# Four layers on one core: Strassen's scheme for the keys and queries of layer 0, first values in layer 3's lone step, and a new order at the end of layer 2

## The chip, the cores and the metric

The kernel runs on one core of a Trainium2 chip. The core has a matrix engine (TensorE, PE in the profile; PEld is its weight load), a vector engine (VectorE, DVE), a scalar engine (ScalarE, ACT), GpSimd (POOL) and SyncE (SP), which here issues the DMA transfers. Each engine works through its own queue in order, and the queues wait for one another by semaphores. Matrix products go into PSUM, everything else lies in SBUF. The metric is the time of one execution on the device in microseconds (us), lower is better.

## The reference

The input x has 4 images of 512 channels and 64 x 64 pixels, float32. Four layers follow one another, each keeping the shape:

```python
# layer 0: attention over the 4096 pixels, D = 64
t = einsum('oc,bchw->bohw', w_qkv, x)            # key, query, value: 64 rows each
attn = softmax(einsum('bdk,bdq->bkq', key, query), axis=1)
x0 = scale * einsum('oc,bchw->bohw', w_out, einsum('bdk,bkq->bdq', value, attn)) + x
# layer 1: 8 experts, mixed per image by a router of the mean over pixels
rw = sigmoid(x0.mean(axis=(2, 3)) @ router_w.T + router_b)
out = relu(bn(conv1x1(x0, mix(w1, rw)))); out = relu(bn(conv3x3(out, mix(w2, rw))))
x1 = relu(bn(conv1x1(out, mix(w3, rw))) + x0)
# layer 2: linear attention
Q, K, V = softplus(Wq x1 + bq), softplus(Wk x1 + bk), Wv x1 + bv
norm = 1.0 / einsum('bnm,bm->bn', Q, K.sum(-1) + EPS)
x2 = x1 + gamma * einsum('bnm,bmc,bn->bcn', Q, einsum('bmn,bcn->bmc', K, V), norm)
# layer 3: 1024 projected channels, half of them scanned along rows and columns
gate, scan = split(einsum('bchw,oc->bohw', x2, w_proj) + b_proj)
x3 = x2 + gamma * gate * sigmoid(cumsum_discounted(cumsum_discounted(scan, rows), columns))
```

Layer 0's projection is the matrix product of the 128 key and query rows (512 channels deep) with the 4096 pixels of an image.

## The kernel before, in words

The program goes through the four images ("batches") one after the other, and in each through `layer0` to `layer3`. An image is held in SBUF as four "pairs" `xs[0]` to `xs[3]` of 1024 pixels; each pair is a tile of 128 partitions by 4 channel blocks (`kc`) by two halves of 512 pixels. Five such places exist (`xpool`); the fifth serves in turn as part of attention's ring, for expert weights, and for layer 3's weights. PSUM is used in two forms: `pair_psum` (three buffers of two banks) and `bank` (two buffers of one bank). SBUF buffers rotate too: `four`, `block` and `bigp`.

PE's program order is the order of the code everywhere, since the whole loop lies in a manual schedule for PE. DVE's order is that of the code where `tc.manual_schedule` names DVE (parts of layers 0, 1 and 2) and in layer 3, where it is so for ACT too. Elsewhere a scheduler orders DVE and ACT by their dependences.

**Layer 0** (L191 to L408). `project_in` (L206) multiplies a 64-column piece of `wqkv_sb` with a pair, the two halves of 512 pixels into the two 64-partition halves of a bank, side by side in the array. Per pair the loop at L220 issues keys and queries (`kq`), four ACT copies of the keys into both partition halves (L229), a DVE copy of the queries (L230), the values (`vv`), a DVE copy (L234) and, one pair later, four transposes of them (L215). Then attention runs in groups: scores (L248), exponentials by ACT into a ring of tiles (L251), running sums by DVE (L256), and products with the values (L263) one group behind. The mean over pixels that the router needs comes for pairs 2 and 3 from ACT activations into a `junk` tile with an accumulated sum (L325). At the end out-products (L307) and additions of the result to x (`add_out`, L312) alternate with the mixing of expert weights.

**Layer 1** (L410 to L527) mixes the remaining expert weights (`mix`, and `mix_by_expert` on DVE, which is called at its start for `ex10`) and runs the three convolutions; `conv3` ends in DVE additions to x (L518).

**Layer 2** (L529 to L693). `features(w, pair)` makes key (w = 1) or query (w = 0) features of two pairs in PSUM (L543); `softplus` (L547) takes ACT's Abs, Relu (`pos`, L552), Exp and Ln and DVE operations. `key_transpose` (L571) turns the keys, `move` (L583) turns pieces of x by eight transposes (L588) and a copy, and `products` (L595) multiplies the two into `g` (L605), with moves and products alternating one by one. `normed` (L637) makes the denominators of one pair: a product of the queries with `kbd` (L640), a reciprocal (L642), a multiplication (L645). After the products come a copy of `g` to `gsb` by ACT (L664), a fold of the two halves by PE (`gk`, L668), another ACT copy (`gt`), the product with Wv (L677) and `kv` by DVE (L678). `value_product` (L687) and `value_add` (L692) then give x2 piece by piece; all but the first four pieces of them are spread over layer 3.

**Layer 3** (L717 to L906) computes its projection already by Strassen's scheme over blocks of 2 x 2: seven products per block, sums of x (`sum_x`, L748) and of the weights ahead of them, a copy of one product into the bank of another as its start value (`seed`, L774), and copies `e2`, `e3` (L778). It runs in nine steps of one loop (L866): in step i the scan half of tile i ("s"), the gate half of tile i − 1 ("g") and the late work of the last tile ("l": scans along rows, a turn, scans along columns, a sigmoid) are interleaved by the table `steps` (L856). Step 0 has no gate half and the last step no scan half: the last is the "lone step", with a table of its own, `last_steps` (L861). A pair of the next image is loaded every second step (L905). The last additions go out by `add_x` (L848) and a DMA on SP.

At the start the four pairs of batch 0 are loaded, pair 0 in four pieces (L86), and then the other constants. GpSimd scales `wv_sb` and `bv_sb` (L112, L113); `kbd`, a 128 x 128 block matrix, is cleared (L130); `bn_s` and its kin are made from the parameters (L136 to L145).

Of the kernel before, what the change touches and what calls it, by code (L numbers as in the profile page):

```python
# [45 lines left out]
def unshifted(ctx: ExitStack, tc: tile.TileContext, fits, x, wqkv_t, wout_t, router_t,  # L46
# [6 lines left out]
    xpool = ctx.enter_context(tc.tile_pool(name="xpool", bufs=5))  # L53
# [26 lines left out]

    def load_pair(b, pr):

        t = xpool.tile([P, KC, 2 * NB], F32, tag="x", name=f"x_{b}_{pr}")
        src = x[b, :, pr * 2 * NB:(pr + 1) * 2 * NB].rearrange("(kc p) n -> p kc n", p=P)
        if b == 0 and pr == 0:
            for kc in range(KC):  # L86
                nc.sync.dma_start(t[:, kc, :], src[:, kc, :])
        else:
            nc.sync.dma_start(t, src)
        return t  # L90
# [4 lines left out]
    xs = [load_pair(0, pr) for pr in range(NPAIR)]  # L95
    prm_sb = const.tile([P, NPRM], F32, tag="prm", name="prm_sb")
# [32 lines left out]
    kbd = const.tile([P, P], F32, tag="kbd", name="kbd")  # L129
    nc.gpsimd.memset(kbd, 0.0)  # L130

# [33 lines left out]
    def load_experts(b, j, n, pool, tag, pack=True):  # L165
        if pack:
            ex = pool.tile([P, n, 4, 2, P], F32, tag=tag, name=f"ex_{b}_{j}")
            nc.sync.dma_start(ex, packed[:, j:j + n])
        else:
            ex = pool.tile([P, n, E, P], F32, tag=tag, name=f"ex_{b}_{j}")  # L170
            nc.sync.dma_start(ex, experts[j:j + n].rearrange("n p e c -> p n e c"))
        return b, j, n, ex
# [18 lines left out]
    def layer0(b, xs):  # L191
# [8 lines left out]
        ring4 = bigp.tile([P, 4, 2, NB], F32, tag="big", name=f"ring_{b}")  # L200
        ringx = xpool.tile([P, 4, 2, NB], F32, tag="x", name=f"ringx_{b}")
        ring = [ring4[:, i] for i in range(4)] + [ringx[:, i] for i in range(4)]
        ring += [four(f"ring_{b}_{i}") for i in range(8, RING)]
        pool_acc = small.tile([P, KC, NPAIR], F32, tag="pool_acc", name=f"pool_{b}")

        def project_in(y, col0, pr):  # L206
            for kc in range(KC):
                for h in range(2):
                    nc.tensor.matmul(y[h * D:(h + 1) * D, :], wqkv_sb[:, kc, col0:col0 + D],  # L209
                                     xs[pr][:, kc, h * NB:(h + 1) * NB], start=kc == 0, stop=kc == KC - 1)  # L210

        def v_transpose(pr, vv, vsb):
            tr = vv[:, 1, :].rearrange("p (j c) -> p j c", c=P)
            for j in range(TPB):
                nc.tensor.transpose(tr[:, j, :], vsb[:, j * P:(j + 1) * P], ident)  # L215
            t0 = pr * 2 * TPB
            nc.vector.tensor_copy(
                vt[:, t0:t0 + 2 * TPB, :].rearrange("p (h j) d -> p j h d", h=2),
                tr.rearrange("p j (h d) -> p j h d", h=2))

        pend = None
        for pr in range(NPAIR):
            kq = pair_psum(f"kq_{b}_{pr}")
            project_in(kq[:, 0, :], 0, pr)
            project_in(kq[:, 1, :], D, pr)
            for h in range(2):
                n0 = (2 * pr + h) * NB
                for to in range(2):
                    nc.scalar.copy(key[to * D:(to + 1) * D, n0:n0 + NB], kq[h * D:(h + 1) * D, 0, :])  # L229
            nc.vector.tensor_copy(qry[:, pr * NB:(pr + 1) * NB], kq[:, 1, :])  # L230
            vv = pair_psum(f"vv_{b}_{pr}")
            project_in(vv[:, 0, :], 2 * D, pr)
            vsb = block(f"vsb_{b}_{pr}")
            nc.vector.tensor_copy(vsb, vv[:, 0, :])  # L234
            if pend is not None:
                v_transpose(*pend)
            pend = (pr, vv, vsb)
# [84 lines left out]
        junk = four(f"junk_{b}")  # L322
        for pr in range(NPAIR - 2, NPAIR):
            for kc in range(KC):
                nc.scalar.activation(flat(junk), xs[pr][:, kc, :], AF.Copy, accum_out=pool_acc[:, kc, pr:pr + 1])  # L325
# [3 lines left out]
        for g, group in enumerate(groups):  # L329
            for i in group:  # L330
                scores(i)
            if g == 0:
                v_transpose(*pend)
# [36 lines left out]
        with tc.manual_schedule(engines={mybir.EngineType.DVE}):  # L370
# [30 lines left out]
            for m in range(1, KC):  # L401
                add_out(pr, m, ys[m])
            for m in range(KC):
# [3 lines left out]
        return wcq, sel, rw, ex4, ex7, ex10  # L407

    def layer1(b, xs, wcq, sel, rw, ex4, ex7, ex10):
# [5 lines left out]
        mix_by_expert(wc, rw, ex10)  # L415
# [23 lines left out]
        v14 = xpool.tile([P, 4, HW // 4], F32, tag="x", name=f"v14_{b}")  # L439
# [89 lines left out]
    def layer2(b, xs, sums_of_six, mix_last, conv2, conv3, wcq, qs):  # L529

        ks = small.tile([P, NPAIR], F32, tag="ks", name=f"ks_{b}")
        g = bank(f"g_{b}", (P, C))
# [4 lines left out]

        def features(w, pair):
            z = pair_psum(f"z_{b}_{w}_{pair[0]}")
            for i, pr in enumerate(pair):  # L540
                for kc in range(KC):
                    for h in range(2):
                        nc.tensor.matmul(z[h * D:(h + 1) * D, i, :], wqk_sb[:, kc, w * D:(w + 1) * D],  # L543
                                         xs[pr][:, kc, h * NB:(h + 1) * NB], start=kc == 0, stop=kc == KC - 1)
# [37 lines left out]

        def move(pr, j):  # L583
# [11 lines left out]
        def products(pr, between=()):  # L595
            between = list(between)
            for j in range(TPB):
                t = pr * TPB + j
                if j + 2 < TPB:
                    move(pr, j + 2)  # L600
                elif between:
                    between.pop(0)()
                xt = moved.pop(0)
                for h in range(2):
                    nc.tensor.matmul(g[h * D:(h + 1) * D, :], kts[pr][:, j, h * D:(h + 1) * D], xt[:, h, :],  # L605
                                     start=t == 0, stop=t == NPAIR * TPB - 1)
# [18 lines left out]
        conv3(2, h2[2])  # L625
        rest = features(0, (0, 1))
        with tc.manual_schedule(engines={mybir.EngineType.DVE}):
            key_transpose((0, 1))
            rest()()
        for step in ahead(0):  # L630
            step()
        conv3(3, h2[3])
        products(0, ahead(1))
        weights[2]()
        features(1, (2, 3))()()
        products(1, ahead(2))
        rest = features(0, (2, 3))  # L637
        def normed(pr, between=None):
            den = bank(f"den2_{b}_{pr}")
            nc.tensor.matmul(den, kbd, qs[:, pr, :], start=True, stop=True)  # L640
            nrm = block(f"nrm_{b}_{pr}")
            nc.vector.reciprocal(nrm, den)  # L642
            if between:
                between()
            nc.vector.tensor_tensor(qs[:, pr, :], qs[:, pr, :], nrm, ALU.mult)  # L645

        with tc.manual_schedule(engines={mybir.EngineType.DVE}):
# [4 lines left out]
            for h in range(2):  # L652
                r = slice(h * D, (h + 1) * D)
                nc.vector.tensor_scalar(kbd[r, r], ones[r, 0:D], ksum[r, :], 1e-6, ALU.mult, ALU.add)
            key_transpose((2, 3))
            rest = rest()
            normed(0)
            rest()
        products(2, ahead(3))

        normed(1)
        products(3, [lambda: normed(2)])
        g_sb = block(f"gsb_{b}", (P, C))
        nc.scalar.copy(g_sb, g)  # L664

        gk = pair_psum(f"gk_{b}")
        for kc in range(KC):
            nc.tensor.matmul(gk[:, 0, kc * P:(kc + 1) * P], g_sb[:, kc * P:(kc + 1) * P], fold,  # L668
                             start=True, stop=True)
        gt = block(f"gt_{b}", (P, KC, P))  # L670
        nc.scalar.copy(gt, gk[:, 0, :].rearrange("p (kc c) -> p kc c", c=P))
        kvp = gk[:, 1, :]
        kv = small.tile([P, C], F32, tag="kv", name=f"kv_{b}", bufs=1)

        def make_kv():
            for kc in range(KC):
                nc.tensor.matmul(kvp, gt[:, kc, :], wv_sb[:, kc, :], start=kc == 0, stop=kc == KC - 1)  # L677
            nc.vector.scalar_tensor_tensor(kv, bv_sb, ksum, kvp, ALU.mult, ALU.add)  # L678

        with tc.manual_schedule(engines={mybir.EngineType.DVE}):  # L680
            normed(3, make_kv)
# [11 lines left out]
        return value_product, value_add, weights, wcq  # L693

    def load_quarters(b):
# [3 lines left out]
        sx = xpool.tile([P, 4, 2, 2, 2 * P], F32, tag="x", name=f"sx_{b}")  # L699
# [17 lines left out]
    def layer3(b, xs, value_product, value_add, weights, wcq):  # L717
# [32 lines left out]
        class Block:  # L750
# [3 lines left out]
            def __init__(self, kind, i):  # L754
# [5 lines left out]
                self.e = {}  # L760

            def product(self, k):
                if k == 1:
# [63 lines left out]
        class Gates(Block):  # L827
# [18 lines left out]
            def add_x(self, i):  # L846
# [10 lines left out]
                 ("s5", "l turn 0", "a"), ("g5", "l columns 1"),  # L857
# [4 lines left out]
        last_steps = (("g1", "g seed", "l rows 1", "l rows 0"), ("g5",), ("g6", "g copy_out 2", "l turn 1"), ("g2",),  # L862
                      ("g7", "g copy_out 3", "l columns 1", "g fourth", "l turn 0", "l columns 0", "l sigmoid 1",
                       "l sigmoid 0"), ("g4",), ("g3", "g third", "g first", "g second"))
        ys = [(pr, m) for pr in range(1, NPAIR) for m in range(KC)]
        nxt = []  # L866
        with tc.manual_schedule(engines={mybir.EngineType.DVE, mybir.EngineType.Activation}):
            for m in range(KC):
                value_add(0, m, value_product(0, m))
                if m == 1:  # L870
                    sum_x(0, 0)
            for part in range(1, 4):
# [3 lines left out]
            for i in range(len(tiles) + 1):  # L876
                who = {"l": last, "s": Sums(1, i) if i < len(tiles) else None, "g": Gates(0, i - 1) if i else None}
                made = None
                for step in steps if who["s"] else last_steps:
                    for what in step:  # L880
# [11 lines left out]
                        elif name == "a":  # L892
                            if made:
                                value_add(*made, y)
                                made = None
                        elif name == "t":
# [470 lines left out]
```

## Time and profile before

Three runs took 2716.63, 2718.47 and 2719.44 us. The profiled execution has a span of 2717.1 us, with a mean granted TensorE clock of 0.997.

| what | where | busy us in the span | mean ns of one |
|---|---|---|---|
| scores | PE L248 | 469.1 | 603 |
| running sums | DVE L256 (two ring forms) | 381.7 + 205.5 | 1223 |
| keys and queries | PE L209, kq | 116.2 | 607 |
| reciprocals of layer 2 | DVE L642, 16 of them | 53.7 | 3356 |
| key copies | ACT L229 | 37.0 | 579 |
| mean over pixels | ACT L325 | 33.9 | 1058 |

A row of the profile's groups gives the line, the engine, the operation, what it writes and reads, the shapes, how often it comes, the busy time and the mean of one, and then the idle time of the engine in front of the group and what ended it. Matmuls in float32 show two records each, and their records overlap, so the time of a run of matmuls is read from the start of one run to the start of the next in the timeline. In the list of waits a row names the waiting engine and line, the engine and line that ended the wait, and then the total, the number of waits and the longest.

### The profile page before, as it was taken

To read this page: it belongs to the slowest core of one execution; us is meant where nothing else is said; L and a number is where in the kernel's file an instruction comes from. 1 tells how busy PE (TensorE), PEld (TensorE's weight loads), DVE (VectorE), ACT (ScalarE), POOL (GpSimd) and SP (SyncE) were. 2 spreads that over 40 slices of the span, in tenths; PEclk is the share of its full clock that TensorE was granted. 3 is DMA by queue.
4 is the path that set the end of the run, shared out by engine and by line. 5 is a ranking of instruction groups with operands and counts; after the bars stand their busy time and mean duration, and the time that the engine had idled before them with its cause. 6 is when DMAs were issued, how large, how long until landed. Compare 5 with 4: busy or idle time off the path is not lost.

```text
span 2717.1 us, 25649 instructions
## 1 busy us (share of the span) xinstructions
PE 2667.3 (98%) x10046; PEld 1114.7 (41%) x10046; DVE 1961.2 (72%) x2197; ACT 1306.6 (48%) x1483; POOL 10.7 (0%) x26
## 2 busy tenths in 40 slices
PE   8999999999999999999999999999999999999998
PEld 3333364344333345444433334544443333554443
DVE  2688766787468876678747778667874777866787
ACT  4544354445555535345555453535555555352545
POOL 1000000000000000000000000000000000000000
PEclk9999999999999999999999999999999999999999
DMA  5000200021200020002220002001121000200011
GB/s 188 1 1 0 101 31 1 16 108 74 82 1 1 1 101 31 1 24 101 78 78 1 1 1 101 32 0 60 64 108 47 1 1 1 101 31 1 31 47 48
DMA packets 34545, 115.15 MB, mean 42 GB/s; under 512 B 2928, under 2 KB 12144, under 8 KB 32880
## 3 DMA queue, kind: packets, MB, share of 16 engines
q1 hardware_dynamic: 34416, 113.43, 11.1%
q8 instruction: 81, 1.33, 0.2%
q14 instruction: 48, 0.39, 0.0%
HBM read 79.86 MB, written 33.55 MB: 42 GB/s over the span
## 4 chain that ended last, share of the span: by engine, by line
PE 86%; DVE 9%; ACT 2%; DMA 1%; issue 1%; SPq 1%; DVEq 0%; ACTq 0%
PE s L248 17%; PE av L263 17%; PE sx L769 14%; PE zy L769 11%; PE c L444 4%; PE kq L209 4%; PE c L493 3%; PE c L516 2%; PE z L543 2%; PE wv L687 2%; PE vv L209 2%; PE g L605 2%; PE xtr L588 2%; PE c2e L493 2%; PE y L307 1%
## 5 line engine op out<-in xcount | busy, mean ns | idle before, releaser
L248 PE MATMUL s<-qv,key 64*128 64x512 f32 x2048 | 469.1, 603 | 1.8 <-ACT ring L251 1.8
L256 DVE TENSOR_TENSOR acc<-acc,ring 128x1024 f32<-128x1024 f32 x312 | 381.7, 1223 | 100.7 <-ACT ring L251 71.9
L251 ACT ACTIVATE ring<-s 128x1024 f32<-128x1024 f32 x336 | 317.7, 1038 | 224.1 <-PE s L248 224.0
L263 PE MATMUL av<-ring,qv 128*64 128x512 f32 x1344 | 304.5, 595 | 0.0
L248 PEld LDWEIGHTS s<-qv,key 64*128 64x128 f32 x2048 | 189.4, 187 | 274.8 <-issue 173.2
L256 DVE TENSOR_TENSOR acc<-acc,ringx 128x1024 f32<-128x1024 f32 x168 | 205.5, 1223 | 102.8 <-ACT ringx L251 90.2
L251 ACT ACTIVATE ringx<-s 128x1024 f32<-128x1024 f32 x176 | 172.1, 1040 | 207.0 <-PE s L248 207.0
L769 PE MATMUL sx<-t,sx 128*128 128x512 f32 x512 | 236.9, 597 | 0.0
L263 PEld LDWEIGHTS av<-ring,qv 128*64 128x64 f32 x1344 | 93.3, 137 | 198.6 <-issue 198.6
L263 PE MATMUL av<-ringx,qv 128*64 128x512 f32 x704 | 167.2, 598 | 0.0
L774 ACT COPY zy<-sx 128x512 f32<-128x512 f32 x64 | 36.5, 570 | 240.1 <-PE sx L769 230.6
L819 DVE TENSOR_TENSOR_SCAN t<-sx,t 128x512 f32<-128x512 f32 x128 | 148.8, 1210 | 1.7
L769 PEld LDWEIGHTS sx<-t,sx 128*128 128x128 f32 x512 | 95.9, 190 | 127.8 <-issue 121.1
L808 ACT COPY t<-s 128x1024 f32<-128x1024 f32 x64 | 127.2, 1994 | 40.5 <-DVE s L802 40.5
L778 ACT ACTIVATE e<-sx,prm_sb 128x512 f32<-128x512 f32 x128 | 86.9, 686 | 123.8 <-PE sx L769 123.8
L802 DVE TENSOR_TENSOR_SCAN s<-wc,s 128x512 f32<-128x512 f32 x128 | 146.0, 1204 | 0.0
L825 ACT ACTIVATE s<-t 128x1024 f32<-128x1024 f32 x64 | 125.5, 1987 | 1.0 <-DVE t L819 0.9
L769 PE MATMUL sx<-t,wq 128*128 128x512 f32 x256 | 117.0, 598 | 7.5 <-ACT e L778 7.5
L209 PE MATMUL kq<-x,wqkv_sb 128*64 128x512 f32 x512 | 116.2, 607 | 6.3 <-DMA x<-in_x_dram 5.6
L769 PE MATMUL zy<-t,wq 128*128 128x512 f32 x256 | 118.7, 604 | 2.5 <-ACT zy L774 2.5
L769 PE MATMUL zy<-x,wq 128*128 128x512 f32 x256 | 116.2, 594 | 0.0
L769 PE MATMUL sx<-x,wq 128*128 128x512 f32 x256 | 116.2, 594 | 0.0
(195 smaller groups left out, 3390.0 us busy)
## 6 DMA issues: line engine op xcount, KB each, us to landing
out_dram<-s SPq DMA_DIRECT2D x64, 512.0 KB, 2.6
x<-in_x_dram SPq DMA_DIRECT2D x15, 2048.0 KB, 8.5
ex<-in_packed_dram SPq DMA_DIRECT2D x8, 1536.0 KB, 6.3
ex<-in_packed_dram SPq DMA_DIRECT2D x4, 2048.0 KB, 7.9
ex<-in_experts_dram SPq DMA_DIRECT2D x4, 2048.0 KB, 7.9
wq<-in_wproj_t_dram SPq DMA_DIRECT2D x32, 256.0 KB, 4.5
ex<-in_experts_dram SPq DMA_DIRECT2D x4, 1536.0 KB, 7.1
x<-in_x_dram SPq DMA_DIRECT2D x4, 512.0 KB, 6.3
```

What stands on the lines that cost most here:

```text
L209: nc.tensor.matmul(y[h * D:(h + 1) * D, :], wqkv_sb[:, kc, col0:col0 + D], xs[pr][:, kc, h * NB:(h + 1) * NB], start=kc == 0, stop=kc == K ...
L248: nc.tensor.matmul(s[:, h, :], key[r, kt * P:(kt + 1) * P], qry[r, pr * NB:(pr + 1) * NB], start=True, stop=True)
L251: nc.scalar.activation(p, s, AF.Exp)
L256: nc.vector.tensor_tensor(accs[pr], accs[pr], p, ALU.add)
L263: nc.tensor.matmul(avs[pr][h * D:(h + 1) * D, :], vt[:, kt, :], ring[i % RING][:, h, :], start=kt == 0, stop=kt == NT - 1)
L444: nc.tensor.matmul(y[:, h, :], wc[:, kc, :], xs[pr][:, kc, h * NB:(h + 1) * NB], start=kc == 0, stop=kc == KC - 1)
L493: nc.tensor.matmul(y[:, lo - a:hi - a], u, v[:, lo:hi], start=dy == 1, stop=dy == 2)
L769: nc.tensor.matmul(y, w[:, c, self.kind, self.j * P:(self.j + 1) * P], v[:, c, :], start=c == 0 and k in (1, 5), stop=c == 1, skip_group_c ...
L802: nc.vector.tensor_tensor_scan(self.half(i, h), along[:, self.j + 2 * i, :], self.half(i, h), 0.0, ALU.mult, ALU.add)
L808: nc.scalar.copy(self.t[i].rearrange("p (w r) -> p w r", w=W), self.s[i].rearrange("p (r w) -> p w r", w=W))
L819: nc.vector.tensor_tensor_scan(th, down[:, i, :], th, 0.0, ALU.mult, ALU.add)
L825: nc.scalar.activation(self.s[i].rearrange("p (r w) -> p w r", w=W), tw, AF.Sigmoid)
```

## The change

The diff has five parts.

- Keys and queries of layer 0 are computed by Strassen's scheme over two pairs at once, the weights and the pixels in 2 x 2 blocks: seven products in the place of eight (class `Projections`, which keeps the steps as lists of words, as layer 3 does). `sum` makes sums of x (t5, t6, t7, t4 for pairs 0 and 1; n5 to n4 for pairs 2 and 3), `sum_weights` those of the weights, and "seed", "e2", "e3", "c11", "c12", "c21" and "c22" are the copies and additions around the products. Values are projected, copied (by ACT now) and turned in between.
- The value projection of the next image's pair 0 (v0) goes into the lone step of layer 3, and its sums t5 and t7 into step 7. The order of g1 and g5 in the lone step is exchanged. The last pair of the next image is loaded inside the lone step, into the fifth place. In batch 0, pair 1 is loaded in four pieces too.
- The activations for the mean over pixels write in place and are issued from inside the attention groups' code; `mix_by_expert` for `ex10` is called at the end of layer 0, after the `add_out` calls.
- The end of layer 2: `move` and `products` in twos; one moved piece in single banks (`move_by_halves`); the key features of pairs 2 and 3 right after `conv3(3)`; denominators of two pairs in 32-row tiles with one reciprocal (`invert`) and a product that spreads them (`divide`); weight sums later; `kv` in two halves.
- The query features of pairs 2 and 3 are cut into quarters: two lie around the copies of `g`, two after it, and they, their softplus and their division (`left`) are carried out in layer 3's first values and steps (`first_steps` and the word "q").

```diff
+    class Projections:
...
+        def steps(self, b):
+            first = "v1 cp01 v2 5 1 seed t6 t4 n5 6 e2 2 c11 n6 tr01 7 e3 c22 v3a n7 4 c21 3 c12 n4"
+            if b == 0:
+                first = "zero v0 1 seed t5 v1 cp01 t6 5 2 c11 t7 t4 n5 6 e2 n6 tr01 v2 7 e3 c22 v3a n7 4 c21 3 c12 n4"
+            return first.split(), "5 1 seed 6 e2 2 c11 v3b cp23 7 e3 c22 tr23 4 c21 3 c12".split()
...
+                elif step.isdigit():
+                    k = int(step)
+                    to = y if k in (1, 6, 7, 4) else zy[:, 0 if k == 2 else 1, :]
+                    for c in range(2):
+                        for h in range(2):
+                            nc.tensor.matmul(to[h * D:(h + 1) * D, :], self.w[k][:, c, :],
+                                             self.term(xs, pair, k, c)[:, h * NB:(h + 1) * NB],
+                                             start=c == 0 and k in (1, 5), stop=c == 1,
+                                             skip_group_check=k not in (1, 5))
+                elif step == "seed":
+                    nc.scalar.copy(zy[:, 0, :], y)
...
-        junk = four(f"junk_{b}")
-        for pr in range(NPAIR - 2, NPAIR):
-            for kc in range(KC):
-                nc.scalar.activation(flat(junk), xs[pr][:, kc, :], AF.Copy, accum_out=pool_acc[:, kc, pr:pr + 1])
+
+        def pool(pr, kc):
+            xm = xs[pr][:, kc, :]
+            nc.scalar.activation(xm, xm, AF.Copy, accum_out=pool_acc[:, kc, pr:pr + 1])
...
+            if 1 < g < 2 + 2 * KC:
+                pool(NPAIR - 2 + (g - 2) // KC, (g - 2) % KC)
...
                 add_out(pr, m, ys[m])
+            mix_by_expert(wcq, rw, ex10)
...
+        def invert(pair):
+            den = bank(f"den2_{b}_{pair[0]}")
+            for i, pr in enumerate(pair):
+                nc.tensor.matmul(den[32 * i:32 * (i + 1), :], kbd, qs[:, pr, :], start=True, stop=True,
+                                 tile_position=(0, 32 * i))
+            inv = block(f"inv_{b}_{pair[0]}")
+            nc.vector.reciprocal(inv[0:D, :], den[0:D, :])
+            return inv
...
+            g_sb = block(f"gsb_{b}", (P, C))
+            nc.scalar.copy(g_sb, g)
+            gt = block(f"gt_{b}", (P, KC, P))
+
+            late = (0, (2, 3), pair_psum(f"z_{b}_0_2"))
+            feature_part(*late, 0, 0, 2)
...
+        left = [lambda: feature_part(*late, 1, 0, 2), lambda: feature_part(*late, 1, 2, 2),
+                lambda: left.append(softplus(*late)), lambda: left.pop()(),
+                lambda: left.append(invert((2, 3))), lambda: divide((2, 3), left.pop())]
...
-        last_steps = (("g1", "g seed", "l rows 1", "l rows 0"), ("g5",), ("g6", "g copy_out 2", "l turn 1"), ("g2",),
+        first_steps = (("s1", "s seed", "q"), ("s5", "q"), ("s6", "s copy_out 2"), ("s2", "s first", "q"),
+                       ("s7", "s copy_out 3", "s fourth", "y"), ("s4", "s third", "a", "d"), ("y", "a", "q"),
+                       ("s3", "s second"))
+        last_steps = (("g5", "l rows 1", "l rows 0"), ("g1", "g seed"), ("g6", "g copy_out 2", "l turn 1"), ("g2",),
                       ("g7", "g copy_out 3", "l columns 1", "g fourth", "l turn 0", "l columns 0", "l sigmoid 1",
-                       "l sigmoid 0"), ("g4",), ("g3", "g third", "g first", "g second"))
+                       "l sigmoid 0", "v"), ("g4",), ("g3", "x", "g third", "g first", "g second"))
```

## The prediction

> **What bounds the kernel now.** I read the engines' busy times first, then the chain that ended last, then TensorE's (PE's) waits, then the timelines of the stretches that the diff touches.
>
> ```profile
> PE 2667.3 (98%) x10046; PEld 1114.7 (41%) x10046; DVE 1961.2 (72%) x2197; ACT 1306.6 (48%) x1483; POOL 10.7 (0%) x26
> PE 86%; DVE 9%; ACT 2%; DMA 1%; issue 1%; SPq 1%; DVEq 0%; ACTq 0%
> ...
> L209 PE MATMUL kq<-x,wqkv_sb 128*64 128x512 f32 x512 | 116.2, 607 | 6.3 <-DMA x<-in_x_dram 5.6
> ```
>
> PE is busy 98% of 2717.1 us at a full clock and its program order is fixed, so time is won in two ways: fewer matmuls, or less waiting in that order. The third line holds the key and query projections.
>
> ```profile
> PE sx L769 <- ACT e L778: 7.5, 12, 0.8
> PE kq L209 <- DMA x<-in_x_dram: 5.6, 1, 5.6
> PE xtr L588 <- ACT pos L552: 3.9, 4, 1.1
> PE wv L687 <- DVE kv L678: 3.7, 4, 0.9
> PE wo_t L161 <- DVE wot_sb L159: 3.2, 1, 3.2
> PE gk L668 <- ACT gsb L664: 2.7, 4, 0.7
> PE zy L769 <- ACT zy L774: 2.5, 4, 0.7
> PE y L307 <- DVE x L312: 2.4, 4, 0.6
> ```
>
> Total, times and longest of each wait: all of PE's waits come to some 37 us, and those with 4 occurrences happen once per batch. The timeline around layer 3's lone step and the projections of the next batch:
>
> ```profile
> 677.30 1.99 PE L769 MATMUL zy<-t,wq 128*128 128x512 f32 x4 [0.66 <-ACT zy L774]
> ...
> 685.21 1.99 PE L769 MATMUL sx<-t,wq 128*128 128x512 f32 x4 [0.78 <-ACT e L778]
> ...
> 688.87 7.09 PE L209 MATMUL kq<-x,wqkv_sb 128*64 128x512 f32 x32
> 695.79 3.60 PE L209 MATMUL vv<-x,wqkv_sb 128*64 128x512 f32 x16
> ...
> 732.28 2.00 PE L248 MATMUL s<-qv,key 64*128 64x512 f32 x8
> ...
> 744.94 0.65 PE L263 MATMUL av<-ring,qv 128*64 128x512 f32 x2
> ```
>
> Between 688.87 and 732.28 PE never waits: 43.4 us of pure matmuls, while DVE is busy 12.6 and ACT 21.4 us.
>
> **What the Trainium skill says.** "TensorE: Matmul & The Clock Gate", Part 3 (The mechanism): matmuls in different tiles of the array run together, but start and end in strict program order. The trace agrees: two 64-column matmuls of 512 take 7.02/16 = 0.44 us against 0.43 for one full one (3.43 us for 8), and one late operand stops all behind it. "SBUF — State Buffer", Terms: DVE and GpSimd share a port pair and the loser blocks. Here a DVE multiply of one column (L142) took most of 2.97 us beside POOL's 5.44 us scaling of wv_sb (L112). "VectorE: DVE Perf Modes", First, the fixed hardware budget: a reciprocal repeats its divide eight times; the trace has 3.36 us (L642) against 0.69 for a copy of the same size. "PSUM — Partial Sum Buffer", The four PSUM rules: a matmul without the start flag adds only where an earlier one has written; no trace here isolates it. Batch 0's extra "zero" matmul sets that up.
>
> **The change, part by part** (per batch, times of the trace's first batch).
>
> *Seven products for eight.* Over two pairs, eight half-products of 1.72 us (four 64-column couples of 0.43) become seven, so two per batch go: 3.43 us, 13.7 in all. To be paid: on DVE 16 tile sums of 1.23 us (19.7 us; four lie in layer 3), on ACT and DVE seeds, e2, e3 and additions at 0.57 to 0.69 each.
>
> *First values in the lone step.* 3.43 us of PE work covers the e3 wait (0.78 plus a restart); with g5 ahead of g1 the seed wait shrinks too. Walking the queues, layer 3 plus the moved work ends at 691.07 instead of 688.87 + 3.43 = 692.30: −1.2.
>
> *From there to the scores.* Unwaited, the new order needs 24.0 (14 half-products) + 10.3 (values 1 to 3) + 2.0 (transposes) = 36.4 us, so scores could begin near 727.5. I find these waits: 1.1 before product 5 (its PSUM slot is released by DVE's leftover of layer 3, which ran until 695.6 before); 0.6 to 0.85 at each of two seeds, where product 6 accumulates into the bank that ACT reads and only the matmuls between could cover; about 1.25 before product 4 of the second half, since ACT's queue has a mean (1.06 + 0.19, in place, waiting for the pair's other readers) right before e3; 0.4 for another ahead of the seed; shape changes and copies 0.5. Scores begin at 732.2, the first value product at 744.6 against 744.94. So I take −0.3 per boundary, three times: −1. With only the two seed waits it is −3.4; with means and copies stacked up in ACT's queue +2.
>
> *Start of batch 0.* No lone step, sums in the projection, x1 in four DMAs on SP. A zero matmul (0.86), ACT's bn_s chain waiting on prm (landing at 27) ahead of e3, DVE sums beside POOL's 7 us: scores at 54.3 instead of 52.16, +2. Bounds: −3 (Strassen's gain unspoilt) and +6 (the whole POOL span lost).
>
> *SP and the spare place.* The next batch's last pair was issued at 696.18 and landed at 704.60. It now goes into the place whose last reader is product 3 of the lone step, so near 691 with a landing near 699.5; its first reader, n5, stands behind DVE's leftover, four small weight sums and t6, t4 (4 × 1.23), about 701.5: nothing, and up to 1 us if output stores hold SP's queue.
>
> *Means in place.* Eight of 1.25 us move within ACT's queue; in attention ACT has 5.8 of a 10.7 us group, so nothing there; the projection has been charged.
>
> *mix_by_expert after the last additions.* Out of DVE's way it ends the L307 wait: 2.4 in the list, with restarts −0.7 per batch, −2.8. Conv1, which needs its output, still comes behind two other mixes. The other bound is 0.
>
> *Layer 2.* The stalls of the reordered end are
>
> ```profile
> 409.11 1.09 PE L588 MATMUL xtr<-ident,x 128*128 128x128 f32 x8 [1.10 <-ACT pos L552]
> ...
> 466.95 1.16 PE L668 MATMUL gk<-fold,gsb 128*128 128x128 f32 x8 [0.69 <-ACT gsb L664]
> ...
> 473.47 3.71 PE L687 MATMUL wv<-wc,kv 64*128 64x512 f32 x16 [0.92 <-DVE kv L678]
> ```
>
> and, counted as PE time beyond 0.43 us per matmul: 1.26, 0.58 (conv's x), 0.86, 1.09 and 0.53 us: 4.3. Moves and products in twos halve the changes of tile shape (0.05 to 0.19 each): 0.7. The late query features (two halves of 1.7) lie over the gsb and gt copies (0.58 each). So the first value product of layer 2 comes at 463.1 instead of 473.47, −10.4, of which 5.3 is moved on (3.43 of features, 1.9 of denominators and their spreading): net −5.0.
>
> *What layer 3 takes back.* Its first steps now carry that work, a softplus and one reciprocal. In the first step e3 stops waiting (−0.9) but s7 waits 0.75 behind ACT's Ln in front of e2: step 1 starts at 485.85 instead of 493.21. In step 1, g1 waits 0.45 for a bank held by the reciprocal, the spread adds 0.95, and it waits 1.95 for a pair buffer that DVE frees after a row scan (1.2 each); one old wait of 0.5 goes. −7.36 + 0.45 + 0.95 + 1.95 − 0.5 = −4.5; the walk in full steps ends at −4.6. Two reciprocals instead of four (−6.7 us of DVE) and the weight sums put after the first division lie beside PE's moves and products: nothing. Bounds: −7.5 with none of the new waits, 0 with the first steps bound by DVE. Four batches: −18.6.
>
> *Tail.* The last batch ends in the same DVE work of the lone step: 0, ±0.5.
>
> Sum: −18.6 − 2.8 − 1 + 2 = −20.4 against this execution's own 2717.1. Three other runs gave 2716.63 to 2719.44, median 2718.47, 1.4 above the span: 2698. Runs differ by 2.8, so 0.2% (5.4 us) is about what can be told from no change.
>
> **Rivals.**
>
> *R1, the projections pay too.* DVE has 30 us free there, so its 12 sums may run ahead and all but the seed waits vanish: 3 × (−3.4) − 3 − 18.6 − 2.8 = −34, 2684. For: no wait today in that stretch. Against: product 6 really follows the seed copy.
>
> *R2, the projections cost.* +3 per boundary and +6 at the start: −18.6 − 2.8 + 9 + 4 to 6, about −8, 2710. For: 8 means of 1.25 us share ACT's queue with six copies that PE waits for. Against: ACT was half idle.
>
> *R3, slower: ACT's queue in the second half.* A mean writes x in place, so it waits for DVE's n4/n7 and for products reading that tile, and everything behind it in order (seed, e2, e3, keys) waits as well. Eight make 10.0 us per batch; my walk lets PE see 1.65. It decides once PE sees over 5.1 more per batch, 6.8 of the 10: then 2719 and up; if all are seen, −20.4 + 4 × 8.4 = +13, 2732. Against: four of the eight stand behind key copies that nothing urgent follows.
>
> *R4, layer 2's gain is only moved.* If layer 3's first steps become DVE-bound, its waits return what was won: −2.8 − 1 + 2, 2716. The moved DVE work is 1.2 + 1.2 + 1.4 + 3.4 + 1.2 = 8.4 us; from 493 to 557 DVE is busy 50.5 of 64, so it fits on the whole.
>
> **How the numbers follow.** My forecast 0.55 (own range 2690 to 2704), R1 0.20, R2 0.14, R4 0.05, R3 0.06. Range 2684 to 2711: it leaves out the outer half of R1's spread and of R2's and all of R3 and R4, about 2 in 10. Faster by over 0.2% 0.89, within 0.05, slower 0.06.
>
> **What would show it.** Right: the key-query line falls to 448 matmuls (and one zero); L209-like time from 116 to about 102; waits on pos, gsb, kv and L312 gone; step 1 of layer 3 about 7 us earlier in batch 0, its pair wait near 2 us; seed waits of 0.6 to 0.9 twice per batch; scores of batch 1 at 728.7 (732.3 + 2 − 0.7 − 4.6 − 0.3). Wrong: projections over 45 us with waits on ACT (R2, R3), under 40 (R1), or layer 3's first two steps long with DVE full (R4).

## The result: 2698.97 us against 2718.84

Six runs of the changed kernel had a median of 2698.97 us (2698.69 to 2700.49), six of the kernel before 2718.84 (2716.63 to 2720.49); the ratio is 0.9929, with a 95% interval of 0.9916 to 0.9942. The profiled execution has a span of 2698.4 us, 18.7 less than before. The forecast was 2698.

The page of the changed kernel, its busy times and the chain that ended last, and from its groups the largest of the key and query products and layer 2's reciprocals:

```profile
PE 2650.6 (98%) x10048; PEld 1114.0 (41%) x10048; DVE 2013.2 (75%) x2270; ACT 1318.2 (49%) x1511; POOL 11.8 (0%) x26
...
PE 89%; DVE 5%; ACT 4%; DMA 1%; issue 1%; SPq 0%; DVEq 0%; ACTq 0%
```

```profile
L296 PE MATMUL kq<-ring,kqw 128*64 128x512 f32 x128 | 32.3, 627 | 7.5 <-ACT kqz L301 7.5
...
L753 DVE RECIPROCAL inv<-den 64x512 f32<-64x512 f32 x8 | 26.7, 3339 | 0.0
```

PE has 16.7 us less to do and is as full as before. The six groups of L296 hold 448 records (128 and five times 64) where L209 had 512; the first of them already shows 7.5 us of waiting for the seed copies. The reciprocals are 8 instead of 16 at an unchanged price. PE's waits (line waiting, line that ended it, total, number, longest):

```profile
PE kq L296 <- ACT kqz L301: 7.5, 7, 2.8
PE nrm L760 <- DVE x L827: 4.7, 4, 1.2
PE kqz L289 <- DVE wqkv_sb L103: 4.4, 1, 4.4
PE kq L296 <- ACT e L304: 3.8, 5, 0.8
PE s L354 <- ACT ring L357: 3.4, 4, 0.9
PE wo_t L175 <- DVE wot_sb L173: 3.3, 1, 3.3
PE sx L904 <- ACT e L913: 2.9, 9, 0.8
PE sx L904 <- ACT zy L909: 2.5, 4, 0.7
PE kqz L296 <- DVE qv L315: 1.8, 1, 1.8
```

The waits on pos, gsb, kv and the last additions of layer 0 are gone. New are those at the seeds and at e3 of the projections (L301, L304) and at the product that spreads the reciprocals (L760); the scores' wait for the exponentials (L357) grew from 1.8 to 3.4 us. To see what each is worth I cut both traces into stages by the first PE instruction of each kind: first scores, first value product of attention, first matmul of layer 1, first value product of layer 2, last matmul of layer 3. Time in a stage, after minus before, in us:

| image | to scores | to first value product | to layer 1 | to layer 2's values | to the end of layer 3 |
|---|---|---|---|---|---|
| 0 | +4.47 | −0.56 | −0.67 | −11.02 | +9.55 |
| 1 | −3.56 | −0.63 | −0.67 | −11.15 | +9.56 |
| 2 | −3.57 | −0.63 | −0.64 | −10.33 | +9.57 |
| 3 | −4.17 | −0.63 | −0.67 | −10.18 | +6.86 |

Layer 3 of images 0 to 2 contains 3.43 us of value projection that was counted in "to scores" before; image 3 has none. Put together by cause: the start of image 0 +3.9, the mix −2.6, layers 2 and 3 −15.2 (the fourth and fifth columns with 6.86 for each image), the three boundaries with the lone step −5.1, the last DVE work +0.4.

### The profile page after: what moved, and what is told of

The parts are those of the page before. It is cut to its first block, busy times and chain, and to the rows that moved or that the text cites. A ratio compares the mean times of both kernels' runs of the same rounds, so it can differ in the third digit from the quotient of the medians.

```text
span 2698.4 us, 25783 instructions
## 1 busy us (share of the span) xinstructions
PE 2650.6 (98%) x10048; PEld 1114.0 (41%) x10048; DVE 2013.2 (75%) x2270; ACT 1318.2 (49%) x1511; POOL 11.8 (0%) x26
## 4 chain that ended last, share of the span: by engine, by line
PE 89%; DVE 5%; ACT 4%; DMA 1%; issue 1%; SPq 0%; DVEq 0%; ACTq 0%
PE av L369 17%; PE s L354 17%; PE sx L904 14%; PE zy L904 10%; PE z L648 4%; PE c L623 4%; PE c L551 4%; PE c L600 3%; PE wv L822 2%; PE y L413 2%; PE g L724 2%; PE xtr L709 2%; PE kq L296 2%; PE c2e L600 2%; PE vv L252 1%; DVE s L937 1%
## 5 line engine op out<-in xcount | busy, mean ns | idle before, releaser
L357 ACT ACTIVATE ring<-s 128x1024 f32<-128x1024 f32 x336 | 317.1, 1039 | 210.6 <-PE s L354 210.6
L362 DVE TENSOR_TENSOR acc<-acc,x 128x1024 f32<-128x1024 f32 x168 | 205.6, 1224 | 102.5 <-ACT x L357 89.5
L357 ACT ACTIVATE x<-s 128x1024 f32<-128x1024 f32 x176 | 171.7, 1040 | 203.2 <-PE s L354 203.2
L904 PE MATMUL sx<-t,x 128*128 128x512 f32 x512 | 237.7, 598 | 3.3 <-ACT zy L909 2.5
L369 PE MATMUL av<-x,qv 128*64 128x512 f32 x704 | 167.2, 598 | 0.0
L904 PEld LDWEIGHTS sx<-t,x 128*128 128x128 f32 x512 | 95.1, 190 | 133.3 <-issue 117.4
L954 DVE TENSOR_TENSOR_SCAN t<-x,t 128x512 f32<-128x512 f32 x128 | 148.8, 1209 | 1.6
L904 PE MATMUL zy<-x,x 128*128 128x512 f32 x256 | 116.2, 594 | 0.0
L648 PE MATMUL z<-x,wqk_sb 128*64 128x512 f32 x512 | 115.9, 597 | 0.0
```

The lines of the kernel that those rows point to most:

```text
L357: nc.scalar.activation(p, s, AF.Exp)
L362: nc.vector.tensor_tensor(accs[pr], accs[pr], p, ALU.add)
L369: nc.tensor.matmul(avs[pr][h * D:(h + 1) * D, :], vt[:, kt, :], ring[i % RING][:, h, :], start=kt == 0, stop=kt == NT - 1)
L904: nc.tensor.matmul(y, w[:, c, self.kind, self.j * P:(self.j + 1) * P], v[:, c, :], start=c == 0 and k in (1, 5), stop=c == 1, skip_group_c ...
L954: nc.vector.tensor_tensor_scan(th, down[:, i, :], th, 0.0, ALU.mult, ALU.add)
```

## The experiments

There are ten kernels. The profiled spans are compared, since the stages of one trace resolve some tenths of a us; medians are given beside them. A single span can be off by 1 or 2 us: the six of the changed kernel lie between 2696.6 and 2698.4, and the profiled one is the longest.

**e1, layer 2 alone.** In the kernel before: the new layer 2, `first_steps`, the word "q", `kbd` and `spread`, and

```diff
                 add_out(pr, m, ys[m])
+            mix_by_expert(wcq, rw, ex10)
...
-        mix_by_expert(wc, rw, ex10)
```

> The kernel before with the new end of layer 2, its late query features in layer 3's first steps and the moved mix_by_expert; keys, queries, values, means and the lone step as before. My theory (the stages of the two traces): layer 2 and 3 give 15.2 us and the mix 2.7, so a span near 2717.1 - 17.9 = 2699.2, as fast as the whole change. Rival, Strassen's scheme carries its own 13.7 us of matmuls: then the rest of the change is worth only about 5 to 7, and this kernel lands near 2711.

Measured: median 2699.07 (ratio 0.9927, 0.9913 to 0.9941), span 2696.3. By the medians it is as fast as the whole change, and the rival is out. Its stages show −0.67 before layer 1, −11.02, −11.15, −10.33, −10.18 in layer 2 and +6.82 to +6.86 in layer 3, so these parts work alone, just as they do in the whole. They make 17.9 of the 20.8 us; the other 2.9 lie outside these stages: 0.73 in image 0 up to the scores, 1.50 from there to the first value product (a shorter stretch of slow clock, see the last section) and 0.62 at image 3.

**e2, the projections alone.** The changed kernel with the old layer 2, the old first step and the old place of the mix.

> The complement: the new projections, the first values in the lone step, the means in place and the new places for x, with layer 2, layer 3's first steps and the mix as before. My theory: the start of batch 0 loses 3.9 us, three boundaries between images win about 1.7 each, the tail loses 0.4, so a span near 2717.1 - 1 = 2716, no change that can be told from none. Rival (Strassen pays 13.7): near 2704. A third, that the two parts need each other (places, queues): the gains of this run and of the one with layer 2 alone do not add up to the whole 18.7.

Measured: median 2718.66 against 2719.7, ratio 0.9994 (0.9985 to 1.0002), span 2717.3. Strassen's scheme with the moved first values is worth nothing that can be measured. Its stages are those of the whole change at the projections: +4.07 at the start, −3.57 and −0.63 at boundaries, +2.69 in layer 3. Stage by stage the two parts add up, which rejects the third theory (the two spans fall by 20.6 together instead of 18.7, but e1's 1.50 of clock is in that). The 13.7 us of matmuls are saved and given back; the next kernels show where.

**e3, means in attention.** The loop over attention's groups goes under a manual schedule for ACT:

```diff
-        for g, group in enumerate(groups):
...
+        with tc.manual_schedule(engines={mybir.EngineType.Activation}):
+            for g, group in enumerate(groups):
...
```

> The changed kernel with ACT kept in the order of the code in attention's groups, so that the eight means of 1.25 us stand behind the third group's exponentials and later, and none of them in the projection's queue. My theory: the start of batch 0 was lost to four means ahead of the second seed in ACT's queue (PE waits 2.85 us there, and its next product takes 3.5 instead of 1.9 us), and each later boundary lost about 1 us to a mean ahead of e3 and of the seed; attention has room for them. So batch 0's scores come about 5 us earlier and each boundary is 1 us shorter: a span near 2698.4 - 8 = 2690. Rival, the start is lost to DVE beside GpSimd's scaling (the sums n7 took 4.08 instead of 2.35 us): then the scores of batch 0 come at most 1 to 2 us earlier, and the span stays above 2695.

Measured: median 2691.72 (ratio 0.9899, 0.9883 to 0.9914), span 2689.6, 8.8 below the changed kernel. The scores of image 0 come 3.8 earlier (5 were expected), each boundary is 1.07 shorter up to the scores and 0.55 from there to the first value product, attention itself is not longer. The edit fixes the whole order of ACT in attention, but at a boundary ACT's other instructions follow one another as before; only the means have gone. PE, then ACT, in the changed kernel around the second seed of image 0:

```profile
37.83 1.89 PE L296 MATMUL kq<-x,wqkv_sb 128*64 128x512 f32 x8
42.57 3.51 PE L296 MATMUL kq<-ring,kqw 128*64 128x512 f32 x8 [2.85 <-ACT kqz L301]
```

```profile
38.38 1.06 ACT L431 ACTIVATE x<-x 128x1024 f32<-128x1024 f32 x1
39.34 0.19 ACT L431 ACTIVATION_READ_ACCUMULATOR x<-x 128x1 f32 x1
39.56 1.30 ACT L282 COPY key<-key 64x512 f32<-64x512 f32 x2
40.88 1.06 ACT L431 ACTIVATE x<-x 128x1024 f32<-128x1024 f32 x1
41.85 0.19 ACT L431 ACTIVATION_READ_ACCUMULATOR x<-x 128x1 f32 x1
41.94 0.58 ACT L301 COPY kqz<-kq 128x512 f32<-128x512 f32 x1
```

The seed copy takes 0.58 us and its operand has been ready since 39.7, but it starts at 41.94: two key copies, which a mean has made late, and another mean stand ahead of it in ACT's queue. It is 2.85 us of waiting, and then the product takes 3.51 instead of 1.94 us. The granted clock says why (columns: window, its length, then busy time of PE, PEld, DVE, ACT and POOL, the clock, DMA):

```profile
36.00:42.00 6.00, 3.72 (x18) 1.00 (x14) 5.94 (x7) 4.64 (x9) 3.72 (x2) 1.00 0.01 3
42.50:46.00 3.50, 3.43 (x10) 1.08 (x12) 0.10 (x1) 1.09 (x3) 0.00 (x0) 0.53 0.00 0
46.00:52.00 6.00, 6.00 (x34) 2.31 (x30) 0.00 (x0) 5.54 (x10) 0.00 (x0) 1.00 0.00 0
```

After the wait PE runs at 0.53 for 3.5 us. So the start's loss was mostly the means: the rival is left with what e7 shows. In e3 the same wait is 1.68 us, the product behind it takes 1.94.

**e4, the division later.**

```diff
-                 ("s5", "l turn 0", "a", "q"), ("g5", "l columns 1"),
+                 ("s5", "l turn 0", "a"), ("g5", "l columns 1"),
...
-                 ("s2", "l sigmoid 0", "s first"), ("g2", "g first", "t 0 1"),
+                 ("s2", "q", "l sigmoid 0", "s first"), ("g2", "g first", "t 0 1"),
```

> The changed kernel with the division of pairs 2 and 3 (the word q) moved four half-steps later in layer 3's steps, from behind s5 to behind s2. My theory: PE's wait at the spreading product (1.18 us, four times) is for a pair buffer of PSUM that DVE frees late because reciprocal and row scans stand before its value addition; later the queue has drained, so the wait goes: -1.2 to -1.3 per batch, a span near 2693.5. Rival: the wait is one for DVE as such and turns up at the next place where PE needs it (another value product or g6's copy), and the span stays within 1 us of 2698.4.

Measured: median 2690.87 (ratio 0.9896, 0.9881 to 0.9911), span 2689.8, −8.6: more than expected. The first of the stretches is of the changed kernel, the second of e4:

```profile
494.37 1.98 PE L904 MATMUL zy<-t,wq 128*128 128x512 f32 x4
497.53 1.13 PE L760 MATMUL nrm<-inv,spread 32*128 32x512 f32 x4 [1.18 <-DVE x L827]
...
512.46 3.70 PE L904 MATMUL sx<-t,wq 128*128 128x512 f32 x8 [0.33 <-ACT e L913]
```

```profile
501.88 1.88 PE L904 MATMUL zy<-x,wq 128*128 128x512 f32 x4
503.69 1.13 PE L760 MATMUL nrm<-inv,spread 32*128 32x512 f32 x4
504.75 1.98 PE L904 MATMUL zy<-x,wq 128*128 128x512 f32 x4
506.57 3.60 PE L904 MATMUL sx<-t,x 128*128 128x512 f32 x8
510.00 3.60 PE L904 MATMUL sx<-t,wq 128*128 128x512 f32 x8
```

Layer 3 is 1.98 us shorter in each image: the wait at L760 with its restart (1.34) and the later one at e (0.5), which the kernel before had too, are both gone; they make 1.84 of it. No new wait takes their place, so the rival is out. The remaining 0.7 lies in the start of image 0, where runs differ by that much without an edit there.

**e5, the seeds covered.**

```diff
-            first = "v1 cp01 v2 5 1 seed t6 t4 n5 6 e2 2 c11 n6 tr01 7 e3 c22 v3a n7 4 c21 3 c12 n4"
+            first = "v1 cp01 v2 5 1 t6 t4 seed tr01 n5 6 e2 2 c11 n6 7 e3 c22 v3a n7 4 c21 3 c12 n4"
...
-            return first.split(), "5 1 seed 6 e2 2 c11 v3b cp23 7 e3 c22 tr23 4 c21 3 c12".split()
+            return first.split(), "5 1 seed v3b 6 e2 cp23 2 c11 7 e3 c22 tr23 4 c21 3 c12".split()
```

> The changed kernel with work put between the seed and product 6: the transposes tr01 in the first half (images 1 to 3; DVE's order of t6, t4 and n5 around it as before), the value quarter v3b and then its copies in the second half (all images). My theory: PE's waits at product 6 (0.67 and 0.87 us per boundary, 2.85 in batch 0) are just the seed copy with nothing between; covered, they go: -1.5 per boundary and about -2 in batch 0, less 0.2 to 0.4 where e3 loses its cover in front of product 4: a span near 2698.4 - 5.5 = 2693. Rival: behind the seed stands a later chain (ACT's means, DVE's n5, which waits for the last pair's landing), so the wait only moves to product 7, 4 or the scores, and the span stays within 2 us of 2698.4.

Measured: median 2691.56 (ratio 0.9896, 0.988 to 0.9911), span 2689.3, −9.1 (5.5 were expected): −3.8 in image 0 and −1.70 at each boundary. At the boundaries no seed wait is left; e3's wait grew from 0.79 to 1.09. In image 0, 1.14 of the seed wait stays and the clock stays up, so the gain there is larger than the wait covered.

**e6, the first values split.**

```diff
-        last_steps = (("g5", "l rows 1", "l rows 0"), ("g1", "g seed"), ("g6", "g copy_out 2", "l turn 1"), ("g2",),
+        last_steps = (("g5", "l rows 1", "l rows 0"), ("g1", "g seed", "v 0"), ("g6", "g copy_out 2", "l turn 1"), ("g2",),
...
-                       "l sigmoid 0", "v"), ("g4",), ("g3", "x", "g third", "g first", "g second"))
+                       "l sigmoid 0", "v 2"), ("g4",), ("g3", "x", "g third", "g first", "g second"))
...
-                            pro.value(nxt, 0)
+                            pro.value(nxt, 0, int(args[0]), 2)
```

> The changed kernel with the first value projection cut in two halves in the lone step, one behind g1's seed and one where all of it stood, ahead of g4. My theory: the seed wait of the lone step (0.66 us, 0.83 with the restart), which the exchange of g1 and g5 left as it was, is covered, and the other half (1.7 us) still covers e3: -0.8 + 0.3 for two more changes of tile shape, three times: a span near 2697. Rival: the value projection's pair buffer of PSUM is not free that early, so a wait of over 0.8 us turns up at its first matmul and the span does not fall.

Measured: median 2698.5 (ratio 0.9925, 0.991 to 0.994), span 2696.7. The size of the span is as expected but not its source: layer 3 is 0.59 shorter three times, the next stage gives back 0.33 (product 5 now waits 0.23 for ACT's copies of the values), and 1.0 of the fall lies in image 0's start, ahead of the edit. The edit's own worth is 0.8 in all; the medians, 2698.5 and 2698.97, do not tell it from none.

**e7, scaling on ACT.** e3 with `nc.gpsimd.tensor_scalar` on `wv_sb` and `bv_sb` replaced by `nc.scalar.activation(t, t, AF.Copy, scale=col(GAM2))` in attention's first group.

> The kernel with the means kept in attention, and in addition the scaling of wv_sb and bv_sb by ACT in attention's first group instead of by GpSimd beside batch 0's projections. What stays to be told is the rest of the loss at the start. Theory: DVE's n7 sums took 4.08 instead of 2.35 us because GpSimd holds the port they share, and the additions and key copies ahead of the second seed are late by that: batch 0's seed wait falls from 1.68 us to 0 to 0.7, its scores come 1 to 1.7 us earlier, and the span is near 2688 against 2689.6. Rival: n7 is long for another reason (its own source, the last pair's DMA), and nothing moves.

Measured: one run, 2690.28, span 2688.4. The two n7 sums of image 0, in e3 and then in e7:

```profile
34.02 4.08 DVE L244 TENSOR_TENSOR ring<-x 128x1024 f32<-128x1024 f32 x2
```

```profile
34.11 2.34 DVE L241 TENSOR_TENSOR ring<-x 128x1024 f32<-128x1024 f32 x2
```

1.7 us of DVE time return when GpSimd is idle, the seed wait falls from 1.68 to 0.67, and image 0's scores come 0.93 earlier than in e3. All of the 1.7 is in the first of the two sums: in e3 it took 2.95 us and the second 1.21. The first ended at 36.97, while GpSimd's operation is recorded from 31.52 to 37.62, so it was held up, but by this record not until that operation ended (spans on GpSimd are rough). The rival on the source of n7's length is out; its share in the start's loss is about 1 us.

**e8, all together.** The edits of e3 to e7 in one kernel.

> All edits of these experiments in one kernel: means in attention, scaling on ACT, the division later, seeds covered, first values split. If the gains belong to separate stages they add up: 2698.4 - 8.8 (means, measured) - 8.3 (division, measured) - 3.5 (seeds, with less to cover once the means are gone) - 1.5 (lone step) - 1.5 (scaling) = a span near 2675. If they cover the same waits twice, 2680 or more.

Measured: median 2675.59 (2674.33 to 2676.3; ratio 0.9837, 0.9823 to 0.985), span 2673.8. It beats both kernels: 23 us below the changed one, 44 below the one before. The forecast of 2675 had already taken off what is covered twice; the plain sum of the five gains would be 29.4 us, and 24.6 were measured, since e3 and e5 end the same wait in image 0. PE is busy for 2645.4 us, 99%.

**e9, the plain counterpart of e8.** e1 with the edit of e4.

> The kernel of e1 (new end of layer 2 and mix, keys and queries by eight plain products, values and means as before) with the later division of e4. It is the plain counterpart of e8, in which every stage has been relieved. If what Strassen's scheme and the first values in the lone step are worth is hidden only by waits, then e8 should lie below this kernel by about the matmuls saved and the e3 waits: 13.7 + 2 to 3. Theory: this kernel has a span near 2696.3 - 8 = 2688.3, 14.5 above e8's 2673.8. Rival: e8's gains come from the means and from the start alone, and this kernel lands within 6 us of e8.

Measured: median 2691.14 (ratio 0.9899, 0.9883 to 0.9916), span 2687.9. So with the queues relieved the projections, with the first values in the lone step, are worth 14.1 us (2687.9 − 2673.8; 15.6 by the medians); without that they are worth nothing (2717.3 with them against 2717.1, or 2698.4 against e1's 2696.3). That this is near the 13.7 of saved products is in part chance. The stages put 10.5 us between the lone step and the first value product of images 1 to 3, about the saved 3.43 each, and 3.9 into the lone steps; the tail gives back 0.4. Image 0, which saves 3.43 too, gains 0.14 up to the first value product (some 1.4 more are hidden by e8's longer stretch of slow clock). e9 lacks the edits of e3 and e7, but there was little for them to end: apart from the first DMA, the router and layers 2 and 3, its PE waits 1.8 us in all, for exponentials.

**e10, the first values back.**

```diff
-            first = "v1 cp01 v2 5 1 seed t6 t4 n5 6 e2 2 c11 n6 tr01 7 e3 c22 v3a n7 4 c21 3 c12 n4"
+            first = "v0 v1 cp01 v2 5 1 seed t6 t4 n5 6 e2 2 c11 n6 tr01 7 e3 c22 v3a n7 4 c21 3 c12 n4"
...
-                       "l sigmoid 0", "v"), ("g4",), ("g3", "x", "g third", "g first", "g second"))
+                       "l sigmoid 0"), ("g4",), ("g3", "x", "g third", "g first", "g second"))
```

> The changed kernel with the first value projection taken out of the lone step and put at the head of the projections of images 1 to 3. Step of the prediction: in the lone step it saves 1.2 us per image by covering the e3 wait (0.78 and the restart), so without it 2698.4 + 3.6 = 2702. What the stages of the trace say: 0.73 per image (two changes of tile shape of 0.1 each come back as a cost), so 2700.6. Rival: at the head of the projection it covers a wait there (product 5 for its PSUM buffer, 0 us by the trace), and nothing changes: 2698.4.

Measured: median 2702.88 (ratio 0.9942, 0.9925 to 0.9958), span 2701.8. Layer 3 is 1.98 shorter and the next stage 3.27 longer, 1.29 per image.

```profile
683.78 1.98 PE L904 MATMUL sx<-t,wq 128*128 128x512 f32 x4 [0.78 <-ACT e L913]
686.26 1.98 PE L904 MATMUL zy<-x,x 128*128 128x512 f32 x4 [0.49 <-DVE e L968]
```

The span came where the 1.2 put it, but that does not confirm the prediction's 1.2, which was meant against the kernel before. Against that kernel the stages give 0.73: layer 3 grows by 2.70 with 3.43 us of values in it (2.69 in e2). Taking the values out again costs more, 1.29, because the sums t5 and t7 of the next image stay in DVE's queue, and product 3 then waits for DVE (0.49): a wait that the change brings with it and that its values cover.

## Why the prediction was right, point by point

The total, 20.4 us of gain against 18.7 measured, is right in its main cause: the end of layer 2 carries it (e1), and what Strassen's scheme saves is eaten at the transitions (e2), as the forecast had it against R1. The terms were less exact than the sum: layers 2 and 3 gave 3.4 us less than forecast, the boundaries 4.1 more and the start 1.9 less. That these nearly cancel, so that the total is within 2 us, is luck.

- *Layer 2*: −10.4 per image to the first value product, measured −10.2 to −11.15. Right.
- *What layer 3 takes back*: +5.75 expected (−10.4 to −4.65), +6.86 measured; for four images −15.2 instead of −18.6. Step 0 was mis-sized: its wait behind Ln was 0.21 and not 0.75, but I charged nothing for changes of tile shape. From the first value product to step 1 the walk had 22.75 us, the trace has 23.86: the 19.74 of before, 4.29 of moved matmuls (features and a denominator), 1.10 less of waits with their restarts, and 0.93 left over for three late pieces between products of another shape. L822 and the quarter of features behind it start 1.92 us apart where the matmuls alone need 1.72. In step 1 the pair buffer's wait was 1.18 (1.34 with the restart) instead of 1.95 and g1 did not wait.
- *Boundaries*: −1 expected, −5.1 measured, of which 0.6 is a wait of image 3 in the kernel before (PE for a DVE copy, behind ACT's means, which wait for a late DMA) that e1 loses as well. The two seed waits were right (0.67 and 0.87 for 0.6 to 0.85). The wait of 1.1 before product 5 was not there: DVE ends L977 at 697.62 and product 5 starts at 697.68. The mean ahead of e3 cost 0.79, not 1.25. From the end of the lone step to the first value product, where the forecast lost 0.9 per boundary, 0.76 was won.
- *The lone step*: −1.2 expected, −0.73 measured against the kernel before (e10). The e3 wait is covered, but the values bring two changes of tile shape, and the part about the seed failed: the exchange of g1 and g5 left that wait at 0.66, only at another product.
- *Start of image 0*: +2 expected, +3.9 measured. The zero matmul was free here (PE waits 0.2 us for x's landing behind it); GpSimd's share was about 1 us (e7). What was missed is R3's mechanism at this one place: means queued ahead of the second seed, 2.85 us, and 1.6 more of slow clock. The bound of +6 held it.
- *R3 and R2*: the same mechanism at the boundaries is 1.6 us per image (e3), as sized at 1.65, far from the 6.8 at which it decides. The places differ, though: about 0.85 at e3 and 0.2 at the seed instead of 1.25 and 0.4, and 0.55 at the first exponentials, behind means that the forecast held to be harmless. R2's +3 per boundary and R1's −34 are both out by e2 and the stages. *R4*: of layer 2's 11 us, 6.86 return in layer 3, 5.15 of them the moved matmuls themselves; what is left, 3.8 per image on average, is what e1 keeps.
- *Mix*: −2.8, measured −2.6 by the stage, the same in e1.
- *The signs*: the 448 records and the zero product came, with 103.6 us for about 102, and the named waits went. Step 1 of layer 3 came only 3.7 us earlier in image 0, since the start had lost more; counted from layer 1 it is 6.9. The scores of image 1 began at 730.5, not 728.7. From the end of layer 3 to these scores it took 39.9 us, which by the letter (under 40) spoke for R1. It was a poor sign: the forecast itself stood at 41.1.

What stays open: the way to the first scores varies without an edit. e2, e4, e6 and e10, which share the changed kernel's start, are 0.4 to 1.0 us shorter there than it; e1 and e9 are 0.7 and 1.4 shorter than the kernel before. So the +3.9, and what e3 and e5 won in image 0, are known to about 1 us. No experiment took this apart, nor the two lengths of the slow clock below.

## What to carry to other kernels

Fewer matmuls pay only if the new dependences have cover: here 13.7 us of products were saved and lost again to copies of half a microsecond. The share of images 1 to 3 came back (10.5 us, and 3.9 in the lone steps) once other PE work stood between most copies and the product that needs them, and once work with slack (the means) was held out of the queue that those copies share. When two edits lie in separate stages, cut the trace at fixed instructions and read each stage; sums over a whole kernel can be right by cancellation. Here the scheduler, free to order ACT, put means ahead of copies that PE waits for, at some 8 us; so name the order where PE waits on an engine.

## What was not expected of the hardware

A wait of PE of about 3 us costs more than itself. After 2.85 us (the changed kernel, e2 and e4), 3.14 us (e6) and 3.19 us (e10) the next product takes 3.3 to 3.6 us instead of 1.94, with a granted clock of about a half (0.53 in the changed kernel); after 1.82 us or less it takes 1.94. Between 1.82 and 2.85 us no wait was seen. The router's wait does the same, but what it costs varies. The first line is of the kernel before, where it lasts 3.19 us until 62.92, the others of e1, where it lasts 3.18 us until 62.18:

```profile
62.90:69.50 6.60, 6.58 (x20) 4.00 (x22) 1.45 (x2) 1.97 (x2) 0.00 (x0) 0.50 0.00 0
```

```profile
62.20:63.80 1.60, 1.60 (x12) 1.34 (x14) 0.23 (x1) 0.00 (x0) 0.00 (x0) 1.00 0.00 0
63.80:67.20 3.40, 3.40 (x12) 1.38 (x10) 1.22 (x1) 1.79 (x2) 0.00 (x0) 0.50 0.00 0
```

In e1 PE ran on at the full clock for 1.6 us and was slow for 3.4 us; in the kernel before it was slow at once and for 6.6 us. The same wait thus cost 1.5 us less in e1, and likewise in e9. In the other traces the slow stretch has the longer form. Two kernels can differ by that much without an edit; what decides between the two lengths is not shown.

The Trainium skill, "TensorE: Matmul & The Clock Gate", Part 1 (What's actually happening), says that the clock is halved after an idle window of about 3.4 us; the half is confirmed here, while waits of 2.85 us were already enough.
